# Projecting the keys and values of 14 context tiles in an earlier sublayer and keeping them in DRAM

## The chip, the cores and the metric

The kernel runs on one core of a Trainium2 chip. A core has a matrix engine (TensorE, PE in the profile), a vector engine (DVE), a scalar engine (ACT), GpSimd (POOL) and a queue that issues DMAs (SyncE, SP). Each runs its own instructions in a fixed order and waits on semaphores for the others. The time is microseconds on the device for one execution of the whole program; lower is better.

## The reference

A decoder of four layers with three sublayers each, on x of 64 sequences x 64 tokens x 256 channels; after each sublayer, x is layer-normalized with its residual. Sublayers are counted 1 to 12. These matter here:

```python
x = _layernorm(x + _L2_xattn_ref(64, 64, 256, L2_xattn_w, L2_xattn_u, x, ctx_2048), axis=-1)   # 8: a recurrence
x = _layernorm(x + _L2_ffn_ref(x, L2_ffn_weight, L2_ffn_bias), axis=-1)                         # 9: a quantized linear layer
x = _layernorm(x + _L3_attn_ref(x, ...), axis=-1)                                               # 10: self-attention
x = _layernorm(x + _L3_xattn_ref(x, ctx_2048, mask_1xSxS2_ff0, ...), axis=-1)                   # 11: cross-attention

def _L3_xattn_ref(hidden_states, encoder_hidden_states, attention_mask, Wq, bq, Wk, bk, Wv, bv, Wo, qn_w, kn_w):
    NH, NKV, HD = 16, 4, 128
    q = (hidden_states @ Wq + bq).reshape(b, s, NH, HD).transpose(0, 2, 1, 3)
    k = (encoder_hidden_states @ Wk + bk).reshape(b, se, NKV, HD).transpose(0, 2, 1, 3)
    v = (encoder_hidden_states @ Wv + bv).reshape(b, se, NKV, HD).transpose(0, 2, 1, 3)
    q, k = _rmsnorm(q, qn_w), _rmsnorm(k, kn_w)      # k and v then repeated for groups of 4 heads
    ...                                              # softmax(q k / sqrt(128) + mask) v
    return out @ Wo
```

The keys and values of sublayer 11 depend on the context alone, which is an input.

## The kernel before

The 4096 tokens are 8 groups of 4 tiles of 128 tokens (two sequences in a tile). `X[g]` holds the rows of a group, `CT[g]` the context of the group, transposed; both stay in SBUF. Large weights go through one ring of eight slots of 8 KB a partition (`weight`, `big_weight`); a slot is loaded again as soon as its last reader is done, and all loads are issued by SP in a fixed order. On PE the order is that of the Python code (`manual_schedule`); the order on the other engines comes from a scheduler at build time.

`l2_mix` computes sublayers 7 and 8: feed-forward slots (`hidden`, `down`), and beside them, as parts popped from a list `behind`, the recurrence of the group before. A recurrence takes the channels in two halves: keys are transposed (`keys`), a running maximum (`maximum`), exponential factors in the tile `e` on ACT (`factors`), two scans and a division on DVE (`sums`, `outputs`, `divided`). `finish` transposes the result back (`yx`), adds the residual and normalizes. The recurrence of the last group has no feed-forward beside it.

`l3_attentions` then computes sublayers 9 to 11. `linear.first` does sublayer 9 for group 0, whose result everything after waits for; the other groups' share (`parts`) runs inside sublayer 10. Sublayers 10 and 11 are one row of 64 + 64 steps; a step is one tile and half of its heads (`hb`). The stages of a step are spread over four turns of the loop by `do(stage, name)`: the projection of the queries at stage 0, turning queries and keys at 1, scores at 1, turning the probabilities and the values at 2, the output projection at 3. In sublayer 11, the step with `hb == 0` also projects the tile's keys (in `query`) and values (in `late`), in the banks of the queries:

```python
k = projected(cs(g, t), lambda c, n: w.kv[:, 0, c, n], slice(0, 512), w.bk, "k", 2)
```

`projected` is two matmuls of 128 x 512 in two PSUM banks used in turn, and an addition of the bias on DVE. In an even turn of the loop the second half of the queries comes ahead of the scores and the value projection near the end; in an odd turn the second half of the queries stands in that late place. The values are then copied by SP with the two sequences of the tile exchanged (`vs`), and keys are scaled on POOL.

In the trace's names, line 276 is `transpose4`, 270 the power on POOL that ends `rsqrt`, 1658 the matmul of `project`, and 255 and 257 the alternating copies of `copy`.

Of the kernel before, what the change touches and what calls it, by code (L numbers as in the profile page):

```python
# [19 lines left out]
P = 128  # L20
D = 256
S = 64
TG = 4
# [8 lines left out]
class Linear:  # L32
# [65 lines left out]
        ends = dec.normalized_parts(x, x)  # L98
        return [turn, quantized, lambda: tiles(0), lambda: tiles(2), *ends]

    def first(self, pool, bank):

        nc, dec = self.nc, self.dec
        x = dec.X[0]
        ps = [dec.transpose4([x[:, t, c * P : (c + 1) * P] for t in range(TG)], "xt") for c in range(2)]
        self.scales()
        xq = pool.tile([P, 2, NTOK], FP8, tag="xq8", name="xq8", bufs=1)
        y = pool.tile([P, TG, D], BF16, tag="s", name="y8f")
        mv = dec.smallp.tile([P, TG, 2], F32, tag="bnmv", name="bnmv", bufs=4)
        rstd, nb = dec.small(TG, "rstd", bufs=4), dec.small(TG, "nmr", bufs=4)  # L110

        def product(t):
            cols = slice(t * P, (t + 1) * P)
            for c in range(2):
                nc.vector.tensor_scalar(xq[:, c, cols], ps[c][:, cols], self.rxs, None, ALU.mult, saturate=False)
            if t % 2 == 0:
                self.banks = bank("o8").rearrange("p (t d) -> p t d", t=2)
            for c in range(2):
                nc.tensor.matmul(
                    self.banks[:, t % 2, :], xq[:, c, cols], self.wq[:, c, :], start=c == 0, stop=c == 1  # L120
                )
            nc.scalar.activation(y[:, t, :], self.banks[:, t % 2, :], AF.Copy, scale=self.sc)

        def rows(t):
            st = dec.smallp.tile([P, 6], F32, tag="bnst1", name="bnst1", bufs=4)
            r, b = rstd[:, t : t + 1], nb[:, t : t + 1]
            nc.vector.tensor_tensor(y[:, t, :], y[:, t, :], self.bias, ALU.add)
            nc.vector.tensor_tensor(x[:, t, :], y[:, t, :], x[:, t, :], ALU.add)
            nc.vector.bn_stats(st, x[:, t, :])
            nc.vector.bn_aggr(mv[:, t, :], st)  # L130
            dec.rsqrt(r, mv[:, t, 1:2], 1.0, 1e-5)
            nc.vector.scalar_tensor_tensor(b, mv[:, t, 0:1], -1.0, r, ALU.mult, ALU.mult)
            nc.scalar.activation(x[:, t, :], x[:, t, :], AF.Identity, bias=b, scale=r)

        for t in range(TG):
            product(t)
        for t in range(TG):
            rows(t)


class L1Ffn:
# [94 lines left out]
class Decoder:  # L236
# [1133 lines left out]
    def l2_l3(self, ctx):  # L1370

        shared = self.pool(ctx, "l2s", 1)
        linear = Linear(self, shared)
        for body in (self.l2_mix, self.l3_attentions):
            with ExitStack() as part:
                self.psum = self.pool(part, "psum_" + body.__name__, 2, space=PSUM, reuse_waits="tile")
                body(part, linear)

    def l2_mix(self, ctx, linear):
# [20 lines left out]

        nc.vector.tensor_scalar_mul(wqkv[:, :, :D], wqkv[:, :, :D], -1.0)
        es = [self.weight(f"l2x_e{i}").rearrange("p (i n) -> p i n", i=4) for i in range(2)]
        w, u = self.column("l2_w", 2), self.column("l2_u", 2)
        decay = wk.tile([P, 2, NB, S], F32, tag="decay", name="decay", bufs=1)
        for c in range(2):
# [197 lines left out]
        with self.tc.manual_schedule(engines={mybir.EngineType.PE}):  # L1605
            for part in mixing(0):
                part()
            slots = [(g, i) for g in range(self.n_groups) for i in range(HC)]
            parts, behind, done = [], [], []
            for n in range(len(slots) + 2):  # L1610
                if n < len(slots):
                    g, i = slots[n]
                    if i == 0:
                        parts = mixing(g + 1) if g + 1 < self.n_groups else []
                    hidden(g, i)
                if n >= 2:
                    down(*slots[n - 2])
                    if slots[n - 2][1] == HC - 1:
                        behind += [(n + 2, part) for part in recurrence(slots[n - 2][0])]

                        if slots[n - 2][0] == self.n_groups - 2:
                            behind[-1] = (len(slots) + 1, behind[-1][1])

                for _ in range(2 if n < len(slots) - HC else 3):
                    if behind and n >= behind[0][0]:
                        behind.pop(0)[1]()
                if parts:
                    parts.pop(0)()
            for _, part in behind:
                part()  # L1630

    def head_rms(self, wk, ps, out, eps, tag):
# [69 lines left out]
    def big_weight(self, name):  # L1702
# [11 lines left out]
            ws.append(w)  # L1714
        return ws

    def distances(self, pool):

        nc = self.nc
        half = lambda b: slice(b * S, (b + 1) * S)  # L1720
        dist = pool.tile([P, S], F32, tag="dist", name="dist", bufs=1)
        for b in range(2):
            nc.gpsimd.iota(
                dist[half(b)], pattern=[[1, S]], base=0, channel_multiplier=-1, allow_small_or_imprecise_dtypes=True
            )
        nc.vector.tensor_scalar_min(dist, dist, 0.0)
        bias = pool.tile([P, 16, S], F32, tag="bias", name="bias", bufs=1)
        start = 2.0 ** (-(2.0 ** -(math.log2(16) - 3)))
        for h in range(16):
            nc.vector.scalar_tensor_tensor(  # L1730
                bias[:, h, :], dist, start * start**h, self.causal64, ALU.mult, ALU.add
            )
        return bias

    def l3_attentions(self, ctx, linear):
# [7 lines left out]
        with self.tc.manual_schedule(engines={mybir.EngineType.PE}):  # L1743
            one, two = self.l3_attn(wk, steps, linear), self.l3_xattn(wk, steps)
            row = [(one, i) for i in range(n)] + [(two, i) for i in range(n)]
            for i in range(2 * n + 3):
# [30 lines left out]
                else:  # L1777
# [4 lines left out]
                    do(0, "query", 0)  # L1782
                    do(1, "key_turned")
                    do(1, "turn", 1)
                    odd = i % 2
                    if not odd:
                        do(0, "query", 1)
                    do(3, "outputs_turned")
                    do(3, "output")
                    do(1, "scores")  # L1790
                    do(2, "turned")
                    do(0, *(("query", 1) if odd else ("late",)))
                    do(2, "values")
                do(0, "end")
                if i == n - 2:
# [4 lines left out]
    def l3_attn(self, wk, steps, linear):  # L1800
# [3 lines left out]

        nc = self.nc
        EPS = 1e-5
        wq, wkk, wv, wp = (self.big_weight(n) for n in ("l3a_wq", "l3a_wk", "l3a_wv", "l3a_wproj"))
        qw, kw, sw = self.column("l3a_qw"), self.column("l3a_kw"), self.column("l3a_sw")
        both = wk.tile([P, 1], F32, tag="both", name="both", bufs=1)
        nc.vector.tensor_scalar(both, kw, qw, 1.0 / math.sqrt(P), ALU.mult, ALU.mult)  # L1810
# [146 lines left out]
                xts[g + 1] = self.transposed(self.X[g + 1], wk, "xt")  # L1957

        ahead, bank = [], lambda name: self.bank(name, bufs=2)
        linear.first(wk, bank)  # L1960
        bias = self.distances(wk)
        xts[0] = wk.tile([P, 2, NTOK], F32, tag="xt", name="xt")
        return SimpleNamespace(
# [4 lines left out]
    def l3_xattn(self, wk, steps):  # L1968
# [13 lines left out]

        def load():

            w.kv = self.weight("l3x_wkv").rearrange("p (i c n) -> p i c n", i=2, c=2)
            self.load(w.kv[:, 0], ins["l3x_wk"].rearrange("(c p) n -> p c n", p=P))
            self.load(w.kv[:, 1], ins["l3x_wv"].rearrange("(c p) n -> p c n", p=P))
            w.q = self.big_weight("l3x_wq")
            w.bq = self.weight("l3x_bq")
            self.load(w.bq, ins["l3x_bq"].broadcast_to([P, WCOLS]))  # L1990
# [8 lines left out]
            w.o = self.big_weight("l3x_wo")  # L1999

        half = lambda b: slice(b * S, (b + 1) * S)
        xts, zs, tiles, state = {}, {}, {}, {}

        def rms(x, out, name):

            sq = wk.tile([P, 4, P], F32, tag="sq", name="sq")
            nc.scalar.activation(sq, x, AF.Square)  # L2007
            nc.vector.tensor_reduce(out, sq, AX.X, ALU.add)
            self.rsqrt(out, out, 1.0 / P, EPS)

        def projected(lhs, w, cols, bias, tag, bufs):
            ps = self.bank("p", bufs=2)
# [5 lines left out]
        def query(i, u):  # L2018

            g, t, hb = steps[i]  # L2020
            if u == 0:
                state[i, "r"] = self.small(8, "hrq")
                if hb == 0:
                    k = projected(cs(g, t), lambda c, n: w.kv[:, 0, c, n], slice(0, 512), w.bk, "k", 2)
                    r = self.small(4, "hrk")
                    rms(k, r, "k")
                    nc.gpsimd.tensor_tensor(k, k, r.unsqueeze(2).broadcast_to([P, 4, P]), ALU.mult)
                    state[i, "k"] = k
# [7 lines left out]
        def late(i):  # L2036

            g, t, hb = steps[i]
            if hb == 0:
                v = projected(cs(g, t), lambda c, n: w.kv[:, 1, c, n], slice(0, 512), w.bv, "v", 2)  # L2040
                vs = wk.tile([P, 4, P], F32, tag="vs", name="vs")
                for b in range(2):
                    nc.sync.dma_start(out=vs[half(b)], in_=v[half(1 - b)])
                tiles[g, t, "v"] = v, vs
# [81 lines left out]
        def end(i):  # L2126
            g, t, hb = steps[i]
            if (t, hb) == (TG - 1, 0) and g + 1 < self.n_groups:
                rows(g + 1)

            if len(steps) - i in (12, 8):
                ahead.extend(self.l3_prepare(len(self.l3_rows)))
# [4 lines left out]
        cs = lambda g, t: lambda c: self.CT[g][:, c, t * P : (t + 1) * P]  # L2137
        return SimpleNamespace(
            load=load, load_biases=load_biases, load_output=load_output, rows=rows, turn=turn, query=query,
            late=late, key_turned=key_turned, turned=turned, scores=scores, output=output, values=values, end=end,  # L2140
        )

    def ternary(self, name):
# [224 lines left out]
```

## Time and profile before

| | us |
|---|---|
| median of 3 runs | 4365.31 |
| lowest, highest | 4363.7, 4369.8 |
| profiled execution | 4366.71 |
| its span, first to last instruction | 4365.0 |

| engine | busy us | share of the span | instructions |
|---|---|---|---|
| PE (matmuls) | 4079.3 | 93% | 28808 |
| DVE | 3095.2 | 71% | 6239 |
| ACT | 2005.0 | 46% | 3667 |
| POOL | 1465.4 | 34% | 1501 |

The page divides the span into 40 equal slices and shows, for each engine, its busy share of a slice in tenths; a row for PE's granted clock stands below them. Other views list one engine's instructions in order of time (start, duration, line, operation, output <- inputs, and in brackets the idle time before it and what ended that), or the busy time of all engines in chosen stretches. Matmul records of fp32 come in pairs: four records are one accumulation of two 128 x 512 products.

### The profile page before, as it was taken

What the parts mean: (1) busy time and instruction counts of PE and PEld (TensorE: products, weight loads), DVE (VectorE), ACT (ScalarE), POOL (GpSimd) and SP (SyncE); (2) the same over time, 40 slices, a digit from 0 to 9 for tenths busy, and PEclk for the clock granted to TensorE, in tenths of its full rate; (3) what the DMA queues carried; (4) which work ended last, traced back from release to release, by engine and by line L of the source; (5) the groups of instructions that cost most, each with busy time, mean ns of one, the idle gap of its engine ahead of it and who ended that gap; (6) DMA issues with size and microseconds to landing.
All of it is one profiled execution on the core that took longest, in us unless ns stands there. A gap on an engine that the chain in (4) does not pass through costs nothing. (4 is left out here: it accounts for less than half of the span.)

```text
span 4365.0 us, 73891 instructions
## 1 busy us (share of the span) xinstructions
PE 4079.3 (93%) x28808; PEld 2634.9 (60%) x28808; DVE 3095.2 (71%) x6239; ACT 2005.0 (46%) x3667; POOL 1465.4 (34%) x1501
## 2 busy tenths in 40 slices
PE   8889999989988999949999999999989999999898
PEld 5645566666665555526666666666656666666566
DVE  6744548888664687877777777777767777777676
ACT  5556545666423567544444444444422232232343
POOL 4411121332431111125555555555533334333111
PEclk9989998999999999979999999999999999999999
DMA  2200012333200000011111111111130000000000
GB/s 84 66 21 10 1 34 68 75 77 69 60 1 22 0 1 1 29 34 30 25 30 25 30 25 30 25 27 29 29 98 13 11 11 11 11 13 11 8 15 17
DMA packets 99685, 128.26 MB, mean 29 GB/s; under 512 B 14916, under 2 KB 72452, under 8 KB 97928
## 3 DMA queue, kind: packets, MB, share of 16 engines
q1 hardware_dynamic: 99336, 123.53, 11.4%
q8 instruction: 228, 3.74, 0.4%
q14 instruction: 121, 0.99, 0.1%
HBM read 61.87 MB, written 19.42 MB: 19 GB/s over the span
## 5 line engine op out<-in xcount | busy, mean ns | idle before, releaser
L270 POOL TENSOR_TENSOR hrq<-hrq,neg_half 128x4 f32<-128x4 f32 x256 | 258.3, 1009 | 535.6 <-DVE hrq L268 531.1
L270 POOL TENSOR_TENSOR rstd<-rstd,neg_half 128x4 f32<-128x4 f32 (+1 forms) x171 | 149.3, 874 | 716.8 <-DVE rstd L268 648.2
L1153 DVE TENSOR_REDUCE mc<-sq 128x2 f32<-128x512 f32 x512 | 317.2, 681 | 65.5 <-PE sk L1151 64.8
L1159 ACT ACTIVATE e<-sk 128x512 f32<-128x512 f32 x512 | 265.5, 608 | 113.2 <-PE sk L1151 111.8
L1148 PE MATMUL sq<-l1x 32*128 32x256 f32 x2048 | 277.0, 408 | 2.6 <-DVE mc L1153 1.6
L270 POOL TENSOR_TENSOR hrk<-hrk,neg_half 128x4 f32<-128x4 f32 x160 | 188.2, 1176 | 200.7 <-DVE hrk L268 197.5
L1658 PE MATMUL p<-l3a_wq,xt 128*128 128x512 f32 x512 | 244.6, 601 | 11.0 <-DVE v L257 9.9
L1151 PE MATMUL sk<-l1x 32*128 32x256 f32 x2048 | 253.2, 393 | 0.0
L1658 PE MATMUL p<-l3a_wk,xt 128*128 128x512 f32 x512 | 247.1, 605 | 0.0
L1148 PEld LDWEIGHTS sq<-l1x 32*128 32x128 f32 x2048 | 209.6, 195 | 57.3 <-issue 24.7
L1658 PE MATMUL p<-l3x_wq,xt 128*128 128x512 f32 x512 | 242.9, 597 | 0.3 <-DVE k L2015 0.3
L1658 PE MATMUL p<-l3a_wv,xt 128*128 128x512 f32 x512 | 234.0, 599 | 0.4 <-ACT y L94 0.4
L2111 PE MATMUL acc<-l3x_wo,yt 128*128 128x256 f32 x1024 | 232.3, 380 | 2.2 <-DVE yt L257 1.2
L1928 PE MATMUL acc<-l3a_wproj,yt 128*128 128x256 f32 x1024 | 234.0, 382 | 0.2 <-DVE yt L257 0.2
L1928 PEld LDWEIGHTS acc<-l3a_wproj,yt 128*128 128x128 f32 x1024 | 195.5, 191 | 54.0 <-issue 29.2
L2007 ACT ACTIVATE sq<-q 128x512 f32<-128x512 f32 x128 | 80.4, 628 | 296.4 <-DVE q L2015 251.5
L2111 PEld LDWEIGHTS acc<-l3x_wo,yt 128*128 128x128 f32 x1024 | 191.7, 190 | 40.9 <-issue 14.3
L1151 PEld LDWEIGHTS sk<-l1x 32*128 32x128 f32 x2048 | 188.6, 187 | 7.1 <-issue 2.9
L276 PEld LDWEIGHTS qT<-ident,q 128*128 128x128 f32 x1024 | 121.2, 141 | 107.2 <-issue 79.9
L276 PE MATMUL qT<-ident,q 128*128 128x128 f32 x1024 | 157.6, 277 | 12.7 <-ACT xt L255 7.9
L1912 POOL TENSOR_TENSOR hry<-hry,neg_half 128x8 f32<-128x8 f32 x64 | 106.3, 1661 | 183.7 <-DVE hry L1908 183.7
L1187 PE MATMUL ret<-e,vt 128*32 128x256 f32 x2048 | 140.9, 390 | 19.4 <-DVE mc L1153 18.3
(396 smaller groups left out, 10150.8 us busy)
## 6 DMA issues: line engine op xcount, KB each, us to landing
vs<-v SPq DMA_DIRECT2D x320, 128.0 KB
x<-in_x SPq DMA_DIRECT2D x8, 512.0 KB
ct<-in_ctxT SPq DMA_DIRECT2D x8, 512.0 KB
cn<-in_ctx SPq DMA_DIRECT2D x8, 512.0 KB
l1x<-in_ctx SPq DMA_DIRECT2D x128, 32.0 KB
l1x_x<-x SPq DMA_DIRECT2D x8, 512.0 KB
l1x<-l1x_x SPq DMA_DIRECT2D x128, 32.0 KB
l1x_r<-r SPq DMA_DIRECT2D x128, 32.0 KB
```

Of the source, the lines that this page charges most:

```text
L270: nc.gpsimd.tensor_tensor(out, out, self.neg_half[:, :n], ALU.pow)
L276: self.nc.tensor.transpose(ps[:, j * P : (j + 1) * P], blk, self.ident)
L1148: nc.tensor.matmul(ps[:, n, :], x_[rows, j, part], c_[rows, j, :], start=True, stop=True)
L1151: nc.tensor.matmul(ps[:, n, :], c_[rows, j, part], x_[rows, j, :], start=True, stop=True)
L1153: nc.vector.tensor_reduce(mc[new % 2][:, ra + k, 2 * j : 2 * j + 2], ps, AX.X, ALU.max, negate=True)
L1159: nc.scalar.activation(es[rb + k], ps, AF.Exp, scale=scale)
L1187: nc.tensor.matmul(ret[32 * r : 32 * r + 32, :], vt[i % 2][:, lc, 4 * r + j, :], es[r][:, lc, :], start=lc == 0, stop=lc == 1,)
L1658: self.nc.tensor.matmul(ps, lhs(c), w(c, cols), start=c == 0, stop=c == 1 and bias is None)
L1912: nc.gpsimd.tensor_tensor(r, r, self.neg_half[:, :8], ALU.pow)
L1928: nc.tensor.matmul(acc[:, :D], yts[h % 2][:, h // 2, :], wp[n // 8][:, (n % 8) * D : (n % 8 + 1) * D], start=n == 0, stop=n == 15,)
L2007: nc.scalar.activation(sq, x, AF.Square)
L2111: nc.tensor.matmul(acc[:, :D], yts[h % 2][:, h // 2, :], w.o[n // 8][:, (n % 8) * D : (n % 8 + 1) * D], start=n == 0, stop=n == 15,)
```

## The change

A new class `ContextRows` takes 14 of the 32 context tiles, every second one from the fourth on: (0,3), (1,1), (1,3), ... (7,1) as (group, tile). For each it makes two units, keys and values. A unit is the two matmuls, a copy from PSUM to SBUF on ACT, and a write of 256 KB to DRAM by SP, without the bias. `fill(n)` emits the next n units at the place in the code where it is called: 2 after the last feed-forward output, 2 ahead of the last group's recurrence, 17 ahead of its `finish`, 5 in `linear.first` after the transposition of `X[0]` and 2 after its products; 28 in all. The weights for this are loaded early into a ring slot of their own, and again for sublayer 11. The loads of the query and key weights of sublayer 10 stand earlier in the code, those of the value and output weights are where they were, one slot later in the ring.

In sublayer 11 the keys and values of such a tile are loaded from DRAM at the end of the step before and the bias is added on POOL in place. Where a tile's keys and values are loaded, the second half of the queries in its first step moves to the late place.

```diff
+    def fill(self, n, pool, tag, bufs, banks, copy):
+        dec = self.dec
+        while n and self.units:
+            n -= 1
+            g, t, i = self.units.pop(0)
+            ps = dec.bank("kv", bufs=banks)
+            for c in range(2):
+                dec.nc.tensor.matmul(
+                    ps, dec.CT[g][:, c, t * P : (t + 1) * P], self.w[:, i, c, :], start=c == 0, stop=c == 1
+                )
+            out = pool.tile([P, 512], F32, tag=tag, name="kv", bufs=bufs)
+            copy(out, ps)
+            dec.nc.sync.dma_start(out=self.dram[g, t, i], in_=out)
...
         ps = [dec.transpose4([x[:, t, c * P : (c + 1) * P] for t in range(TG)], "xt") for c in range(2)]
+        fill(5)
         self.scales()
...
         for t in range(TG):
             product(t)
+        fill(2)
         for t in range(TG):
             rows(t)
...
+        context.load()
+        fill = lambda n: context.fill(n, wk, "hid", 4, 3, nc.scalar.copy)
...
+                if n == len(slots) + 1:
+                    fill(2)
...
-            for _, part in behind:
+            fill(2)
+            self.l3a_qk = [self.big_weight(name) for name in ("l3a_wq", "l3a_wk")]
+            for k, (_, part) in enumerate(behind):
+                if k == len(behind) - 1:
+                    fill(17)
                 part()
...
-                    odd = i % 2
-                    if not odd:
+                    queries = i % 2 or i >= 2 * n or two.ready(i - n)
+                    if not queries:
                         do(0, "query", 1)
...
-                    do(0, *(("query", 1) if odd else ("late",)))
+                    if queries:
+                        do(0, "query", 1)
+                    if not i % 2:
+                        do(0, "late")
...
-        wq, wkk, wv, wp = (self.big_weight(n) for n in ("l3a_wq", "l3a_wk", "l3a_wv", "l3a_wproj"))
+        fill = lambda n: self.context.fill(n, wk, "q", 3, 2, nc.scalar.copy)
...
+        def ready(i):
+            return steps[i][:2] in context.tiles
+
+        def loaded(i):
+            for k, name in enumerate("kv"):
+                t = wk.tile([P, 4, P], F32, tag=name, name=name, bufs=2)
+                self.load(t.rearrange("p h d -> p (h d)"), context.dram[(*steps[i][:2], k)])
+                state[i, name] = t
+
+        def biased(i, name, bias):
+            t = state.pop((i, name))
+            flat = t.rearrange("p h d -> p (h d)")
+            nc.gpsimd.tensor_tensor(flat, flat, bias, ALU.add)
+            return t
...
+                    if ready(i):
+                        k = biased(i, "k", w.bk)
+                    else:
+                        k = projected(cs(g, t), lambda c, n: w.kv[:, 0, c, n], slice(0, 512), w.bk, "k", 2)
...
+            if hb == 1 and i + 1 < len(steps) and ready(i + 1):
+                loaded(i + 1)
```

The value path in `late` has the same choice between `biased` and `projected`.

More of the change, by code (lines that the diff above doesn't have):

```diff
@@ L99, in parts, with first @@
         return [turn, quantized, lambda: tiles(0), lambda: tiles(2), *ends]
-    def first(self, pool, bank):
+    def first(self, pool, bank, fill):
         nc, dec = self.nc, self.dec
@@ L136, in first, with __init__, load @@
             product(t)
+        fill(2)
         for t in range(TG):
             rows(t)
+class ContextRows:
+    def __init__(self, dec):
+        self.dec = dec
+        tiles = [(g, t) for g in range(dec.n_groups) for t in range(TG)][3::2][:14]
+        self.dram = {}
+        for g, t in tiles:
+            for i in range(2):
+                self.dram[g, t, i] = dec.tc.dram_tile([P, 512], F32, name=f"l3x_kv{i}_{g}_{t}")
+        self.units = list(self.dram)
+        self.tiles = set(tiles)
+    def load(self):
+        self.w = self.dec.keys_values_weight("l3x_wkv0")
+    def fill(self, n, pool, tag, bufs, banks, copy):
[11 more added lines that the diff above has]
+            dec.nc.sync.dma_start(out=self.dram[g, t, i], in_=out)
 class L1Ffn:
@@ L1375, in l2_l3 @@
         linear = Linear(self, shared)
+        self.context = ContextRows(self)
         for body in (self.l2_mix, self.l3_attentions):
@@ L1404, in l2_mix @@
         es = [self.weight(f"l2x_e{i}").rearrange("p (i n) -> p i n", i=4) for i in range(2)]
+        context = self.context
+        context.load()
+        fill = lambda n: context.fill(n, wk, "hid", 4, 3, nc.scalar.copy)
         w, u = self.column("l2_w", 2), self.column("l2_u", 2)
@@ L1715, in big_weight, with keys_values_weight @@
         return ws
+    def keys_values_weight(self, name):
+        w = self.weight(name).rearrange("p (i c n) -> p i c n", i=2, c=2)
+        for i, n in enumerate(("l3x_wk", "l3x_wv")):
+            self.load(w[:, i], self.ins[n].rearrange("(c p) n -> p c n", p=P))
+        return w
     def distances(self, pool):
@@ L1959, in l3_attn @@
         ahead, bank = [], lambda name: self.bank(name, bufs=2)
-        linear.first(wk, bank)
+        linear.first(wk, bank, fill)
+        (wq, wkk), wv, wp = self.l3a_qk, self.big_weight("l3a_wv"), self.big_weight("l3a_wproj")
         bias = self.distances(wk)
@@ L1983, in load @@
         def load():
-            w.kv = self.weight("l3x_wkv").rearrange("p (i c n) -> p i c n", i=2, c=2)
-            self.load(w.kv[:, 0], ins["l3x_wk"].rearrange("(c p) n -> p c n", p=P))
-            self.load(w.kv[:, 1], ins["l3x_wv"].rearrange("(c p) n -> p c n", p=P))
+            w.kv = self.keys_values_weight("l3x_wkv")
             w.q = self.big_weight("l3x_wq")
@@ L2001, in l3_xattn @@
         half = lambda b: slice(b * S, (b + 1) * S)
-        xts, zs, tiles, state = {}, {}, {}, {}
+        xts, zs, tiles, state, context = {}, {}, {}, {}, self.context
         def rms(x, out, name):
@@ L2023, in query @@
                 if hb == 0:
-                    k = projected(cs(g, t), lambda c, n: w.kv[:, 0, c, n], slice(0, 512), w.bk, "k", 2)
+                    if ready(i):
+                        k = biased(i, "k", w.bk)
+                    else:
+                        k = projected(cs(g, t), lambda c, n: w.kv[:, 0, c, n], slice(0, 512), w.bk, "k", 2)
                     r = self.small(4, "hrk")
@@ L2039, in late @@
             if hb == 0:
-                v = projected(cs(g, t), lambda c, n: w.kv[:, 1, c, n], slice(0, 512), w.bv, "v", 2)
+                if ready(i):
+                    v = biased(i, "v", w.bv)
+                else:
+                    v = projected(cs(g, t), lambda c, n: w.kv[:, 1, c, n], slice(0, 512), w.bv, "v", 2)
                 vs = wk.tile([P, 4, P], F32, tag="vs", name="vs")
@@ L2139, in l3_xattn @@
             load=load, load_biases=load_biases, load_output=load_output, rows=rows, turn=turn, query=query,
-            late=late, key_turned=key_turned, turned=turned, scores=scores, output=output, values=values, end=end,
+            late=late, ready=ready, key_turned=key_turned, turned=turned, scores=scores, output=output, values=values, end=end,
         )
```

## The prediction

> **What bounds the kernel now.** I read the page's 40 slices first, then busy time by stretch, then the engines in order of time at the seam and in one tile of the eleventh sublayer.
>
> ```profile
> PE   8889999989988999949999999999989999999898
> ...
> PEclk9989998999999999979999999999999999999999
> ```
>
> TensorE (PE) is at nine tenths nearly everywhere, so the kernel is bound by its matmuls. The one hole is the slice with a 4, where the granted clock is also 7: the seam between the eighth sublayer's last recurrence and the ninth sublayer. Busy time by stretch (columns: PE, weight loads, DVE, ACT, POOL, granted clock, DMA) sets the hole beside the steady part of the eleventh sublayer:
>
> ```profile
> 1854.20:1921.40 67.20, 11.69 (x44) 7.20 (x42) 51.83 (x122) 24.67 (x32) 6.20 (x13) 0.56 0.15 48
> 3240.00:4000.00 760.00, 742.76 (x5264) 500.96 (x5265) 573.41 (x1144) 223.09 (x392) 261.02 (x251) 1.00 0.06 12
> ```
>
> In the hole PE works 11.7 of 67.2 us at a mean clock of 0.56, while DVE works 52: the recurrence is a DVE chain. In the later stretch PE is busy 97.7%, DVE 75%, POOL 34%. PE's row in the hole, then one tile (two steps) of the eleventh sublayer:
>
> ```profile
> 1864.77 2.80 PE L1418 MATMUL tr<-ident,x 128*128 128x128 f32 x8 [3.99 <-ACT x L328]
> 1889.77 0.45 PE L1582 MATMUL yx<-ident,yx 128*128 128x128 f32 x1 [22.20 <-DVE yx L1571]
> 1899.18 1.75 PE L1582 MATMUL yx<-ident,yx 128*128 128x128 f32 x7 [8.96 <-DVE yx L1571]
> ...
> 1921.39 6.21 PE L1658 MATMUL p<-l3a_wq,xt 128*128 128x512 f32 x8 [1.13 <-ACT xt L255]
> ```
>
> ```profile
> 3520.86 0.66 PE L276 MATMUL qT<-ident,q 128*128 128x128 f32 x4
> 3521.35 1.88 PE L1658 MATMUL p<-l3x_wkv,ct 128*128 128x512 f32 x4
> 3523.07 1.88 PE L1658 MATMUL p<-l3x_wq,xt 128*128 128x512 f32 x4
> ...
> 3532.06 1.88 PE L1658 MATMUL p<-l3x_wkv,ct 128*128 128x512 f32 x4
> ...
> 3534.97 0.66 PE L276 MATMUL qT<-ident,q 128*128 128x128 f32 x4
> ...
> 3546.08 0.66 PE L276 MATMUL qT<-ident,q 128*128 128x128 f32 x4
> ```
>
> The first step of a tile, with key and value projection, takes 3534.97 − 3520.86 = 14.11 us, the second 11.11. Bracketless rows did not wait. Starts, not durations, give the price, since matmuls overlap: 3523.07 − 3521.35 = 1.72 us a projection.
>
> **What the change takes away.** For 14 of 32 tiles two projections leave this stage: 14 x 2 x 1.72 = 48.2 us of PE. The shortened first step, 14.11 − 3.44 = 10.67 us, holds the second step's PE work less one group of key transposes (0.43), with the second query in the same late place. The second step already runs unstalled at 11.11, which is why I expect the shortened one to stay on PE. DVE loses 28 bias additions of about 0.68 (19 us); per tile it had 0.754 x 25.22 = 19.0 us and keeps 17.7 in 21.8, 81%. Two covers get thinner: the probabilities were ready on POOL 4.7 us before their transposition in the odd step and 5.9 in the even one; the latter falls to 2.5. The late query's scale needs 5.0 us from its matmul through DVE, ACT, DVE and POOL; the next scores need it 8.9 us after that matmul, so 3.9 remain. Neither is used up, but DVE runs in a fixed order at 81%, and one wait of 0.25 us in a tile seems fair: **+3.5 us** (bounds 0, and 1.5 us a tile or 21).
>
> **What it puts on POOL and SP.** POOL adds 28 biases over two SBUF operands. Its nearest row:
>
> ```profile
> L2074 POOL TENSOR_TENSOR s<-s,smx x64: 1033/1044/1372, 3226.2 to 4051.5; 128x512 f32<-128x512 f32 x64
> ```
>
> 28 x 1.04 = 29 us, or 2.1 a tile; POOL goes from 8.6 to 10.7 in 21.8 us, off the path. The Trainium skill (SBUF, "Who interferes with whom") speaks against it: a DVE instruction with two SBUF inputs and a GpSimd one that reads SBUF exclude each other for a whole instruction. By that rule each addition could hold one DVE operation up to 1.04 us: 29 us of DVE, which at 19.8 of 21.8 us a tile would leave it almost bound and make the loss about 20 instead of 3.5. By the rows it is mostly POOL that waits: the multiplication above stretches from 1.03 to at most 1.37, while the mask addition on DVE (two SBUF inputs, 64 times) never exceeds 0.69. I take the rows. The value's addition waits for its load; behind it on POOL stand the key's scale and multiplication, which PE wants a step later. The load may go once values two tiles back are read, at the end of the step before; issue to use by an estimate is about 3 us (the seam's 1 MB weight loads take 5.2 to 5.5 from issue to use, of which some 3.3 us moved data, so about 2 fixed and 0.8 for 256 KB). It is covered by most of a step. On SP the 28 loads stand among swap copies that have a step to spare. No cost.
>
> **What it puts into the seam.** 28 units (a projection each, 1.72 us) are 48.2 us of PE in 67 us that PE had mostly free, plus an ACT copy of 0.58 (the row for `k<-tr`) and a 256 KB write each. Their places decide, so I follow ACT's new fixed order:
>
> ```profile
> 1876.49 1.91 ACT L1551 ACTIVATE l2x_e<-l2x_e 128x2048 f32<-128x2048 f32 x1
> ...
> 1900.61 2.00 ACT L1951 ACTIVATE l3a_wproj<-l3a_wproj,l3a_sw 128x2048 f32<-128x2048 f32 x1 [8.80 <-DMA l3a_wproj<-in_l3a_wproj]
> ```
>
> - Before the first exponential ACT now runs one copy and the second half's first Relu (1.06): the half's sums on DVE start 0.6 + 1.06 = 1.7 us later. DVE waited 2.65 us for it and has nothing else, so the last `yx` is ready at 1899.1 + 1.7 = 1900.8.
> - With three banks PE stops at unit 10 (1877) until ACT has finished the exponentials' preparation (1881.6), then runs at 1.72 to unit 21 at 1901.4: 0.6 after `yx`. That 4.6 us gap may halve the clock again (it fell about 4 us after PE stopped at 1854.2), costing 1.7 more; I leave that to the range.
> - The five units behind the transposes wait for copies that stand behind the normalization on ACT; the quantized product starts 2.3 us late. Two more copies go ahead of the last normalization: query projection at 1924.5, 3.1 late.
> - Against it: PE is now warm. The first eight matmuls took 6.21 at half clock; eight such in the same stage at full clock take 3.6. That returns 2.6.
> - The second output weight now takes the slot of the moved weights, so it is loaded only after unit 28 (1921.4) and lands near 1926.9. ACT scales it (2.0) ahead of the first squares, to 1928.9, where the squares began at 1925.9 before. Behind it wait the second query's copy and, through the bank, PE; following both to the first key transposes leaves 0.5 to 1.5.
> - SP: the two value weight loads and the first output weight queue among the writes; the value weight lands near 1892 and is wanted at 1944. Four output buffers allow 6.9 us for a write, against about 3.
>
> Net in the seam **+1.5 us**. Bounds: −3 if the warm clock repays more, +12 if the clock falls, writes come slowly and ACT holds the first step. The early load of the moved weights takes a slot that its last reader leaves before the loads next to it; its DMAs precede results that are used a sublayer later. No cost.
>
> **Sum.** The profiled execution took 4366.7 us (span 4365.0), 1.4 over the median shown. 4366.7 − 48.2 + 3.5 + 1.5 = 4323.5, against the median 4322: I say 4323.
>
> **Rivals.**
> 1. *The shortened step stalls.* For: DVE at 81% in a fixed order, the POOL/DVE exclusion. Against: the second step runs so already. With 1.5 us a tile the 3.5 becomes 21: about 4340.
> 2. *The seam gives part back*, by the clock, slow writes or ACT behind the last weight. For: ACT and SP run in order, and the weight is loaded late. Against: the hole is longer than the work. At +12 instead of +1.5: about 4333.
> 3. *Slower: the late query's scale decides the step.* Its operations on POOL now queue behind key bias, value bias and key multiplication. If these delay it past the 3.9 us left, DVE stands at the scores' scaling with all evacuations behind it, and PE stops on its two projection banks. Each tile loses what exceeds 3.9; beyond 3.9 + 3.44 = 7.3 us a tile the change loses. At 8 us: 14 x 4.1 − 48.2 + 1.5 = +11, 4377. POOL's added 2.1 us a tile are far from it.
> 4. *Nothing moves*: the stage falls back on another bound of the same length. 4366; the step of 11.11 us speaks against it.
>
> **How the numbers follow.** Likeliest 60%, its own range 4315 to 4331; rival 1 19%, rival 2 14%, rival 3 4%, rival 4 3%. The range takes in both milder rivals: 4313 to 4344. Within 0.2% (8.7 us, about what a measurement of this kernel can tell from no change) lies rival 4 alone, beyond it upward rival 3.
>
> **What would show it.** Right: steps with loaded keys start 10.7 us apart in PE's row; the slice with 4 becomes 8 or 9 and its clock 9 or 10; the first query projection runs 8 matmuls in about 3.6; PE's busy sum hardly changes. Wrong: PE waiting on DVE or POOL in those steps, DVE two-input operations above 0.69, a long ACT wait for the second output weight, `yx` transposes well past 1902. A time above 4344 refutes the forecast.

## The result, and the profile after

| | before | after |
|---|---|---|
| median, us (4 runs each, same chip) | 4365.82 | 4338.98 |
| lowest, highest | 4363.7, 4369.8 | 4336.5, 4343.85 |
| profiled execution, us | 4366.71 | 4343.85 |
| its span | 4365.0 | 4342.1 |

The ratio after/before is 0.9939, 95% interval 0.9922 to 0.9956: 27 us faster, where 42 were forecast. The profiled execution of after is the longest of its four, so the profiles differ by 22.9 us only; against the forecast sum for the profiled execution (4323.5) 20.3 us are missing. The question is where they are.

The line of busy times and the slices from the page of after:

```profile
PE 4079.0 (94%) x28788; PEld 2635.7 (61%) x28808; DVE 3092.6 (71%) x6211; ACT 2018.1 (46%) x3695; POOL 1498.3 (35%) x1529
...
PE   8889998989888999989999999999989999999898
...
PEclk9989999999999999999999999999999999999999
```

The slice with the 4 is an 8 now, and its clock a 9. PE does the same work as before (4079.3 us), so the hole was filled and not merely moved. A detail to keep: DVE lost 28 bias additions of 0.68 us, or 19 us, and yet it is busy for 3092.6 us instead of 3095.2. The same two stretches as before, by windows:

```profile
1854.20:1921.40 67.20, 56.14 (x155) 25.91 (x154) 51.01 (x115) 34.49 (x53) 4.11 (x10) 0.97 0.43 152
3240.00:4000.00 760.00, 726.91 (x5316) 501.31 (x5312) 589.11 (x1151) 228.75 (x405) 301.65 (x287) 0.99 0.09 23
```

In the seam PE works 56 us instead of 12, at a clock of 0.97. In the eleventh sublayer it works 726.9 of 760 us instead of 742.8: this stage was limited by PE and is so no longer everywhere. PE's row in the seam:

```profile
1882.40 20.85 PE L168 MATMUL kv<-l3x_wkv,ct 128*128 128x512 f32 x44 [4.26 <-ACT kv L172]
1903.09 1.04 PE L1621 MATMUL yx<-ident,yx 128*128 128x128 f32 x8
...
1925.43 3.70 PE L1703 MATMUL p<-l3a_wq,xt 128*128 128x512 f32 x8 [1.29 <-ACT xt L290]
```

The first query projection starts at 1925.4 instead of 1921.4 and takes 3.70 us instead of 6.21. The first key transposes come at 1936.54 instead of 1934.05: the seam ends 2.5 us later, of which 0.8 were there before its first unit.

Now the steps of the eleventh sublayer. A step is here the stretch of PE's row, one turn of the loop, that holds the step's own projections; it begins with a group of query transposes. I took these starts from both traces, from tile 2 of group 0 on, and sorted the differences of 59 step lengths, after minus before, by tile of the group and step of the tile:

| tile | first step, us | second step, us |
|---|---|---|
| 0 | 0.0 | 0.0 |
| 1 (keys and values loaded in 7 groups) | −24.0 | **+21.4** |
| 2 | +0.5 | +2.4 |
| 3 (loaded in 7 groups) | −25.5 | 0.0 |

The sum is −25.2, where −44.7 was forecast. The shortened steps gain what they should (7 x 3.43 in tile 1). Nearly all that tile 1 gains is given back in one place, its second step. PE's row there, in group 1:

```profile
3337.23 0.66 PE L311 MATMUL qT<-ident,q 128*128 128x128 f32 x4
...
3345.00 1.88 PE L1703 MATMUL p<-l3x_wq,xt 128*128 128x512 f32 x4
...
3347.90 0.66 PE L311 MATMUL qT<-ident,q 128*128 128x128 f32 x4
...
3350.12 0.60 PE L311 MATMUL kT<-ident,k 128*128 128x128 f32 x4
3352.95 0.66 PE L311 MATMUL qT<-ident,q 128*128 128x128 f32 x4 [2.23 <-DVE qT L292]
3353.45 5.31 PE L2189 MATMUL acc<-l3x_wo,yt 128*128 128x256 f32 x16
...
3363.16 0.66 PE L311 MATMUL qT<-ident,q 128*128 128x128 f32 x4
```

The shortened step takes 3347.90 − 3337.23 = 10.67 us, to the digit of the forecast. The next takes 15.26 instead of 11.60: PE waits 2.23 us for a DVE copy, and then sixteen matmuls that take 3.62 us at full clock take 5.31. The view in windows of 1 us says why (the number ahead of the last two is the granted clock):

```profile
3354.00:3355.00 1.00, 1.00 (x5) 0.79 (x4) 0.35 (x3) 0.86 (x2) 1.00 (x2) 0.62 0.00 0
3355.00:3356.00 1.00, 1.00 (x4) 0.80 (x3) 0.77 (x2) 0.00 (x0) 0.78 (x2) 0.50 0.00 0
3356.00:3357.00 1.00, 1.00 (x4) 0.73 (x3) 0.00 (x0) 0.00 (x0) 0.89 (x1) 0.50 0.00 0
3357.00:3358.00 1.00, 1.00 (x5) 0.85 (x4) 0.00 (x0) 0.00 (x0) 0.00 (x0) 0.67 0.00 0
```

From 1.3 us behind the wait on, PE's clock is halved for 3.4 us, which costs 1.7 us more. PE waits 2.2 us for that copy in all seven groups; in four of them the clock falls, in three it does not (those steps are 13.57, 13.56 and 14.64 us).

Why is DVE late? DVE and then POOL in the same tile, and behind them `rstd` and its reader in that place before:

```profile
3341.19 0.87 DVE L303 TENSOR_SCALAR hrk<-hrk 128x4 f32<-128x4 f32 x1
...
3344.67 0.71 DVE L303 TENSOR_SCALAR rstd<-bnmv 128x4 f32<-128x4 f32 x1
...
3347.33 1.38 DVE L342 TENSOR_SCALAR x<-z,bnmv,rstd 128x256 f32<-128x256 f32 x4 [1.36 <-POOL rstd L305]
...
3352.22 0.68 DVE L292 COPY qT<-qT 128x512 f32<-128x512 f32 x1
```

```profile
3340.99 1.04 POOL L2152 TENSOR_TENSOR s<-s,smx 128x512 f32<-128x512 f32 x1
3341.99 1.27 POOL L2080 TENSOR_TENSOR v<-v,biases 128x512 f32<-128x512 f32 x1
3343.22 1.02 POOL L305 TENSOR_TENSOR hrk<-hrk,neg_half 128x4 f32<-128x4 f32 x1
3344.31 1.04 POOL L2102 TENSOR_TENSOR k<-k,hrk 128x512 f32<-128x512 f32 x1
3345.31 1.01 POOL L305 TENSOR_TENSOR hrq<-hrq,neg_half 128x4 f32<-128x4 f32 x1
3346.28 1.01 POOL L305 TENSOR_TENSOR rstd<-rstd,neg_half 128x4 f32<-128x4 f32 x1
```

```profile
3350.90 1.01 POOL L270 TENSOR_TENSOR rstd<-rstd,neg_half 128x4 f32<-128x4 f32 x1 [0.89 <-DVE rstd L268]
...
3351.94 1.38 DVE L307 TENSOR_SCALAR x<-z,bnmv,rstd 128x256 f32<-128x256 f32 x4 [0.52 <-POOL rstd L270]
...
3353.89 0.66 PE L276 MATMUL qT<-ident,q 128*128 128x128 f32 x4
...
3356.97 0.65 PE L276 MATMUL qT<-ident,q 128*128 128x128 f32 x4 [0.27 <-DVE qT L257]
```

Three things meet in this turn of the loop. First, the layer normalization of the group before falls here (statistics, `rstd`, four scalings): its last output comes three turns after the last step of that group, which is the turn of tile 1's first step. Second, POOL's value bias stands in a chain of six operations without a gap, with `rstd` at its end, and DVE, in order, waits 1.36 us for it (0.52 in the same place before). Third, two small DVE operations on 128x4 take 0.87 and 0.71 us instead of 0.16 and 0.17. Each ends within 0.03 us of the end of a large POOL instruction that began before it (3342.06 and 3342.03; 3345.38 and 3345.35). The same operation over the stage, before and then after (smallest, median and largest duration in ns):

```profile
L268 DVE TENSOR_SCALAR hrk<-hrk x29: 152/158/163, 3267.4 to 3995.1; 128x4 f32<-128x4 f32 x29
```

```profile
L303 DVE TENSOR_SCALAR hrk<-hrk x30: 157/740/871, 3268.1 to 3995.8; 128x4 f32<-128x4 f32 x30
```

From 3270 to 4000 us DVE's scaling operations of this kind take 50.9 us instead of 29.6. That is where the 19 us of saved additions went.

But the third thing is not what PE waits for here. POOL takes the results of the two held operations only 1.2 and 0.9 us after they are done, and both end before DVE's wait of 1.36 us: without the hold that wait would be longer, and nothing else. What PE waits for is `rstd`. Before, it ended 1.98 us ahead of the second step (3350.90 + 1.01 against 3353.89) and PE waited 0.27 us; now it ends 0.61 us ahead (3346.28 + 1.01 against 3347.90) and PE waits 2.23. Of the 1.96 us more, 1.37 are the later `rstd`; the other 0.6 are one more DVE operation between it and the copy, a sum of squares of the late second queries. The experiments below change when `rstd` ends, and PE's wait follows it.

### The profile page after: what moved, and what is told of

The parts are those of the page before. It is cut to its first block, busy times and chain, and to the rows that moved or that the text cites. A ratio compares the mean times of both kernels' runs of the same rounds, so it can differ in the third digit from the quotient of the medians.

```text
span 4342.1 us, 74081 instructions
## 1 busy us (share of the span) xinstructions
PE 4079.0 (94%) x28788; PEld 2635.7 (61%) x28808; DVE 3092.6 (71%) x6211; ACT 2018.1 (46%) x3695; POOL 1498.3 (35%) x1529
## 3 DMA queue, kind: packets, MB, share of 16 engines
q14 instruction: 124, 1.01, 0.1%
## 5 line engine op out<-in xcount | busy, mean ns | idle before, releaser
L1703 PE MATMUL p<-l3a_wq,xt 128*128 128x512 f32 x512 | 242.1, 595 | 11.1 <-DVE v L292 9.9
```

Of the source, the lines that this page charges most:

```text
L1703: self.nc.tensor.matmul(ps, lhs(c), w(c, cols), start=c == 0, stop=c == 1 and bias is None)
```

## The experiments

All edits are to the changed kernel unless said otherwise; each median stands beside a kernel before of the same chip, and the ratio is to that one. "The stage" is the sum of the 59 step differences to before in the profile, −25.2 us for the change.

**The seam alone.**

```diff
-        self.tiles = set(tiles)
+        self.tiles = set()
```

> The 28 units are projected and written as in the change, but sublayer 11 does not use them: it projects all keys and values itself, with the loop order of before. This prices the earlier part alone. By the forecast the seam costs 1.5 us: about 4367 us. If the missing 16 us lie in the seam: about 4380. If the warm clock repays more than the delays cost: 4363.

Measured: 4369.04 against 4367.66 us, ratio 1.0002, interval 0.9994 to 1.0010, so +1 us with −3 to +4 around it. The seam's price is about as forecast, and the missing 16 us are not there.

**Other tiles.** Two kernels: tiles 2 and 3 of groups 0 to 6, and the same row one tile later (`[1:15]` for `[:14]`).

```diff
-        tiles = [(g, t) for g in range(dec.n_groups) for t in range(TG)][3::2][:14]
+        tiles = [(g, t) for g in range(dec.n_groups) for t in (2, 3)][:14]
```

> The same 14 tiles' worth of work, but tiles 2 and 3 of groups 0 to 6 in place of tiles 1 and 3. Theory A (the layer normalization of the group before, which falls on DVE in the loop turn of tile 1's first step, finds no room once that step is shortened): the shortened steps of tile 2 take 10.7 us and the step behind each 11.1, tile 1's second step goes back from 15.2 to 11.6, and the 21 us lost there come back: about 4318 us. Theory B (any shortened first step overloads DVE's fixed order, with the bias additions on POOL): the second step of tile 2 stretches to 15 us as tile 1's did, and the time stays at about 4339.

> Tiles 2 and 3 again, but beginning with tile 3 of group 0 and ending with tile 2 of group 7, so that no loaded tile lies in the first turns of sublayer 11, where the kernel with tiles 2 and 3 waited 7.0 us for POOL's probabilities instead of 5.6 and lost 3.7 us over three turns. If that loss came from the two tiles' bias additions on POOL at that place: 3 to 4 us less than with tiles 2 and 3, about 4326. If it came from elsewhere: 4329 again.

Measured: 4329.33 (ratio 0.9911, 0.9897 to 0.9926) and 4328.28 us (ratio 0.9905, 0.9890 to 0.9920). The stage gives −39.2 and −40.9. Tile 2 in PE's row of the second kernel:

```profile
3363.36 0.66 PE L311 MATMUL qT<-ident,q 128*128 128x128 f32 x4
...
3374.03 0.66 PE L311 MATMUL qT<-ident,q 128*128 128x128 f32 x4
...
3377.04 0.66 PE L311 MATMUL qT<-ident,q 128*128 128x128 f32 x4 [0.20 <-DVE qT L292]
...
3385.56 0.66 PE L311 MATMUL qT<-ident,q 128*128 128x128 f32 x4
```

The step behind the shortened one takes 11.53 us, not 15, and the wait for DVE is 0.20 instead of 2.23. The same step, shortened in the same way, is harmless where no normalization falls: theory A stands, B falls. It is about 10 us short of the fall to 4318 that was expected: in the profile of the first kernel the second steps of tile 2 are still 6.0 us longer than before (0.4 in most, and one half-clock stretch), and those of tile 1, in three groups, 4.4. Of the three first turns of sublayer 11 the later row saves 2.85 us in the profile (59.2 instead of 62.05); the times can't tell the two apart.

**The normalization emitted later.**

```diff
-                if t == TG - 1:
+                if t == TG - 1 and g == self.n_groups - 1:
                     self.layernorm(x, z)
...
+            if (t, hb) == (1, 1) and g:
+                self.layernorm(self.X[g - 1], zs[g - 1])
```

> Tiles 1 and 3 as in the change, but the layer normalization of the finished group (statistics, rstd, four scalings) is emitted two turns of the loop later, ahead of tile 2's first step, which still projects keys and values and takes 14.1 us. Theory A: tile 1's second step falls from 15.2 to between 11.1 and 12.5 us, and the time to about 4320 us. Theory B: no change in that step, about 4339.

Measured: 4347.32 us, ratio 0.9950 (0.9936 to 0.9963); the stage gives −20.0. This test missed its aim: the order on DVE is made by the scheduler, which put the statistics and `rstd` back where their input was ready, with the same wait of 1.36 us, and only spread the four scalings between the other operations; PE's wait grew to 2.64 us. It says nothing on A or B.

**The biases left out, and the value bias on DVE.**

```diff
-            nc.gpsimd.tensor_tensor(flat, flat, bias, ALU.add)
+            (nc.vector if name == "v" else nc.gpsimd).tensor_tensor(flat, flat, bias, ALU.add)
```

(The other kernel drops the line; it leaves out the bias of the loaded keys and values.)

> Leaves out the bias of the loaded keys and values, so POOL loses 28 additions of 1.27 us. Theory C (the value bias, which stands on POOL ahead of the key's scale, holds rstd and so DVE): tile 1's second step loses most of its 3.6 us excess, and the time falls by 15 to 20 us, to about 4321. Theory A (DVE is full in that tile whatever POOL does): POOL's chain gets 1.3 us shorter, so at most 7 x 1.3 = 9 us come back, to 4330 to 4335.

> Tiles 1 and 3 as in the change; the bias of the loaded values is added on DVE instead of POOL, that of the keys stays on POOL. DVE gets 14 additions of about 0.69 us, POOL loses 14 of 1.27. Theory C (POOL's chain in tile 1's first step, in which the value bias stands ahead of the key's scale, the late query's scale and rstd, holds DVE): tile 1's second step falls from 15.2 to about 12.9 us as it did without biases, and its half-clock stretch goes: about 4332 us. Theory A (DVE itself is full there): 0.7 us more of DVE in that tile make the step longer than 15.2, and the time 4341 to 4346.

Measured: 4333.65 us without biases (ratio 0.9915, 0.9901 to 0.9930), 4347.23 with the value bias on DVE (ratio 0.9953, 0.9940 to 0.9965, which overlaps the interval of the change). Without biases tile 1's second step takes 12.85 us, as C said, and the stage gives −34.0, the 9 us that A allowed. With the value bias on DVE the step stays at 15.02, where C said 12.9 and A more than 15.2, and tile 3's first step grows from 12.67 to 13.64. Tile 1 of group 1 without biases, then with the value bias on DVE:

```profile
3345.25 1.01 POOL L305 TENSOR_TENSOR rstd<-rstd,neg_half 128x4 f32<-128x4 f32 x1 [0.20 <-DVE rstd L303]
...
3347.58 0.66 PE L311 MATMUL qT<-ident,q 128*128 128x128 f32 x4
...
3351.91 0.66 PE L311 MATMUL qT<-ident,q 128*128 128x128 f32 x4 [1.52 <-DVE qT L292]
```

```profile
3343.82 1.52 POOL L2102 TENSOR_TENSOR k<-k,hrk 128x512 f32<-128x512 f32 x1
...
3346.65 1.01 POOL L305 TENSOR_TENSOR rstd<-rstd,neg_half 128x4 f32<-128x4 f32 x1 [0.20 <-DVE rstd L303]
...
3348.50 0.66 PE L311 MATMUL qT<-ident,q 128*128 128x128 f32 x4
...
3353.31 0.66 PE L311 MATMUL qT<-ident,q 128*128 128x128 f32 x4 [2.00 <-DVE qT L292]
```

Both take an addition of 1.27 us out of POOL's chain, but `rstd` ends only 0.71 and 0.23 us sooner (1.32 and 0.84 us ahead of the second step instead of 0.61), because POOL now waits 0.20 us for DVE's input of it. In both a scaling of the queries is held 1.0 us on DVE ahead of that input; in the second kernel DVE also has the addition (0.68 us), and POOL's key multiplication takes 1.52 us beside it in all 14 places, 1.04 in the change. So POOL's chain and DVE's fixed order limit `rstd` in turn, and a shorter chain on POOL is worth little if DVE pays for it. Neither C alone nor A alone describes this.

**The small scaling on ACT.** This takes the small scalings of the sums of squares off DVE and leaves POOL's operations as they are.

```diff
-            self.rsqrt(out, out, 1.0 / P, EPS)
+            nc.scalar.activation(out, out, AF.Copy, scale=1.0 / P, bias=EPS)
+            nc.gpsimd.tensor_tensor(out, out, self.neg_half[:, : out.shape[-1]], ALU.pow)
```

> The change with one edit: in sublayer 11 the small operation that scales the sums of squares ahead of the power (128x4, a TENSOR_SCALAR on DVE) is done by ACT; POOL's chain, bias additions included, stays. Theory D (these small operations are held on DVE while a POOL instruction runs, 0.74 us instead of 0.16 for the keys' one, and DVE is full in tile 1's turn): DVE loses some 46 us in the stage, tile 1's second step falls from 15.2 to 12.5 us or less, without a half-clock stretch, and the time to about 4325. Theory C (the length of POOL's chain decides): tile 1's second step stays above 13.5, and the time at 4338 or more, since ACT adds a hop to each scale.

> The kernel before, with the small scaling of sublayer 11 on ACT and nothing else. Its DVE has room in every tile; only tile 1's second step (11.6 instead of 11.1 us) can shorten: 8 x 0.5 us or 4 us at most, 4362 to 4366. Much less than 4360 would mean that the small operations were a cost by themselves and not only beside the shortened steps.

Measured: 4329.68 us, ratio 0.9909 (0.9895 to 0.9922), so some 13 us below the change; on the kernel before, the same edit gives 4371.00, ratio 1.0006 (0.9998 to 1.0014), no gain. PE, POOL and DVE of the first in tile 1 of group 1:

```profile
3336.68 0.66 PE L311 MATMUL qT<-ident,q 128*128 128x128 f32 x4
...
3347.35 0.66 PE L311 MATMUL qT<-ident,q 128*128 128x128 f32 x4
...
3351.65 0.66 PE L311 MATMUL qT<-ident,q 128*128 128x128 f32 x4 [1.49 <-DVE qT L292]
3352.15 3.62 PE L2190 MATMUL acc<-l3x_wo,yt 128*128 128x256 f32 x16
```

```profile
3338.57 1.01 POOL L2066 TENSOR_TENSOR hrq<-hrq,neg_half 128x4 f32<-128x4 f32 x1 [6.91 <-ACT hrq L2065]
3339.69 1.04 POOL L2153 TENSOR_TENSOR s<-s,smx 128x512 f32<-128x512 f32 x1
...
3344.99 1.01 POOL L305 TENSOR_TENSOR rstd<-rstd,neg_half 128x4 f32<-128x4 f32 x1
```

```profile
3346.03 1.38 DVE L342 TENSOR_SCALAR x<-z,bnmv,rstd 128x256 f32<-128x256 f32 x4 [1.14 <-POOL rstd L305]
```

PE's wait shrinks to 1.49 us, the clock does not fall in any of the seven groups, and the step takes 12.83 us, a little above the 12.5 expected; the stage gives −37.4. So the edit helps, but the trace does not give theory D's reason. DVE still waits 1.14 us for `rstd`, so DVE's time ahead of it is not what is short. What has moved is the start of POOL's chain: ACT delivers the first sum of squares sooner, POOL has taken its power by the time the next operation's input is there, and the multiplication behind it starts 3.01 us after the step's start (3339.69 against 3336.68) instead of 3.76. From there POOL works without a gap as before, and `rstd` ends 0.74 us sooner. The four kernels side by side, in tile 1:

| kernel | `rstd` ends ahead of the second step, us | PE waits in it, us |
|---|---|---|
| the change | 0.61 | 2.23 |
| value bias on DVE | 0.84 | 2.00 |
| without biases | 1.32 | 1.52 |
| small scaling on ACT | 1.35 | 1.49 |

The two columns add up to 2.84 in each, within 0.02 in all seven groups: DVE does the same work from the end of `rstd` to the copy, and 5.7 us pass until PE goes on. So PE's wait is set by the end of POOL's `rstd`. The 12 us that the stage regains are seven times 0.74 us and four half-clock stretches of 1.7. That the held operations cost time by themselves is not shown: the kernel before gains nothing from the edit, and neither does the kernel with tiles 2 and 3 (below). What is left of tile 1's loss (9.3 of 21.4 us) is the normalization itself and POOL's chain.

**The second queries in their old place.**

```diff
-                    queries = i % 2 or i >= 2 * n or two.ready(i - n)
+                    queries = i % 2 or i >= 2 * n
```

> Undoes one part of the change: in steps with loaded keys and values the second half of the queries stays ahead of the scores, so that nothing stands between the turned probabilities and the values on PE. Where the last turns of the row have nothing there, PE waits 0.73 us for the copy of the probabilities. If only that wait is exposed: 14 x 0.73 us or 10 us, about 4350. If the early place spares DVE's chain in tile 1 instead (the second query's scale is then ready earlier): under 4335.

Measured: 4342.76 us, ratio 0.9940 (0.9928 to 0.9953), the same as the change. Tile 1's shortened step takes 11.42 instead of 10.67 us (the exposed copy, 0.75), and its second step 12.74 instead of 15.26 without a fall of the clock, since two DVE operations fewer stand between `rstd` and the copy (4.6 us from the end of `rstd` to PE's transposes instead of 5.7): both expectations were half right, and they cancel. The reordering brought nothing here.

**Combinations.**

> Tiles 2 and 3 (from group 0's tile 3 on) and the small scaling on ACT. If D holds: tile 2's second step goes from 11.5 to 11.1 us and tile 1's first steps keep the normalization under 14.1, so the stage comes within 5 us of the full 48 us: about 4322. If ACT's hop delays the scales: 4330 or more.

> Tiles 2 and 3 from group 0's tile 3 on, and the bias of the loaded values on DVE. If both effects are separate and DVE has room in tiles 2 and 3: 2 to 4 us below the kernel with the tiles alone, about 4323. If DVE is the tighter one there: equal or up to 5 us above it.

> Tiles 2 and 3 of all eight groups: 16 tiles, 32 units, the four more of them ahead of the transposition of the last recurrence's result. In the traces with 28 units PE runs there without a gap until that result is ready (unit 21 ends at 1903 us, the transposition follows at once). If the hole is full: four units of 1.72 us put everything behind them 6.9 us later, sublayer 11 gets 6.9 us shorter, and with the first two tiles' 3.7 us the time is 4328 to 4332, no gain over 14 tiles. If there is still room: about 4322.

The last kernel's edit is `for t in (2, 3)]` without a limit, and `fill(21)` for `fill(17)`. Measured, in this order: 4328.25 (ratio 0.9907, 0.9894 to 0.9921), 4350.91 (0.9955, 0.9942 to 0.9967) and 4331.53 us (0.9928, 0.9914 to 0.9941). The small scaling on ACT adds nothing once the tiles are 2 and 3: tile 2's second step stays at 11.53 us, where D expected 11.1. The value bias on DVE costs 22 us there, far more than the 5 expected: tile 2's second step grows from 11.5 to 12.4 us and more, and tile 3's first step from 12.7 to 13.6. And the hole is full: with four more units the transposition of the recurrence's result starts 57.0 us after the first unit instead of 48.1 in the change, so 8.8 us later, and the stage gains only 6.5 us more than with 14 tiles (−45.7 against −39.2).

So the kernels with 14 tiles 2 and 3 (4328 to 4329 us) beat both, by 38 to 42 us against before and, by the ratios, 12 to 15 against the change.

## Why the prediction was right, and where it was off

The direction and the mechanism were right, and the time fell in the range, but at the place of the first rival ("the shortened step stalls", about 4340), not of the likeliest case. By its steps:

- **The projections that leave.** −48.2 us was right for the steps themselves: 10.67 us against a forecast of 10.67.
- **The term that failed: +3.5 us for waits in the shortened steps**, "one wait of 0.25 us in a tile seems fair". The runs show 23.0 in the profile, 21.4 of it in tile 1's second step. The working took DVE's mean over the tiles (81%) and asked whether a mean tile has room, and it put POOL's added work "off the path". The normalization's operations don't fall in a mean tile; they all fall in the turn of tile 1's first step, which was one of the two chosen for shortening, and there POOL is on the path: `rstd` stands at the end of its chain, DVE waits for it, and PE for DVE. The trace of before showed the place: tile 1's second step took 11.61 us there and tile 2's 11.11.
- **POOL beside DVE: "I take the rows".** The Trainium skill (SBUF, "Who interferes with whom") names two kinds of DVE instruction that share a port with GpSimd: those with two SBUF inputs, and those in a two-port mode, which `tensor_scalar` can enter; whoever issues first has the port for the whole instruction. I looked at the first kind alone (the mask addition; one of 64 takes 0.82 us after the change, the others 0.69 at most). The second kind is held: of 160 small scalings in sublayer 11, 49 take between 0.35 and 0.87 us (before, 28 of 155 take 0.35), and each of them ends within 0.06 us of the end of a POOL instruction. The prediction put the hold at up to 29 us of DVE by the rule; measured are 50.9 − 29.6 = 21. From this hold the rule's working made a loss of about 20, near the 23.0 above; that agreement is luck, since in tile 1 the hold falls into time that DVE would otherwise wait for `rstd`.
- **What a stall starts.** The sum had no term for PE's clock in sublayer 11. A wait of 2.2 us was followed by half clock for 3.4 us in four groups of seven, 1.7 us each. In the last steps the clock halved too and sixteen matmuls took 5.52 us instead of 3.88, which lost 1.6 more after the stage; the waits there (0.73 and 1.16 us) stand in before as well, without a fall.
- **POOL's additions** took 1.27 us each, not the 1.04 of the row for a multiplication by a broadcast operand.
- **The seam: +1.5 us.** The profile shows +1.7 (2.5 less the 0.8 from before it), and the seam alone +1 in the times. The details held: PE stopped for 4.26 us at 1878 (forecast: 4.6), the first query projection began at 1925.4 (1924.5) and took 3.70 us (3.6). The clock did halve at that stop, from 1883.1 to 1886.5, which the prediction had left to the range; the end of the block of units came at 1903.2 instead of 1901.4.
- **The late place of the second queries** was part of the shortened step's 10.67 us. The gain doesn't depend on it: in the old place the time is the same.
- **The rest.** The three turns at the border of sublayers 10 and 11 became 1.8 us shorter. The sum for the profile: 4323.5 + 19.5 (steps) + 1.0 (seam) − 1.8 + 1.6 = 4343.8, against 4343.85.

Rival 3 named POOL's queue behind the two biases as the danger and the late query's scale as what it delays. The queue was there, but the operation at its end that mattered was the normalization's `rstd`, and the size of the loss was rival 1's.

## What to carry to other kernels

A mean busy share over a stage says little about a step that is to be shortened: list what the other engines do in that very step, above all the work that comes once per group, and take the time out of steps in which the next engine has nothing extra. When work goes to an engine that is off the path on average, look at what else stands behind it in that step and who waits for it: here one operation of 1.0 us at the end of POOL's chain set PE's wait. A DVE operation that grows beside POOL is a loss only where DVE does not wait afterwards anyway. And when PE's wait nears 2 us, add the half clock that may follow it: in four of seven groups here it made 2.0 us of loss into 3.6.

## What was not expected of the hardware

A gap of 2.2 us in PE's work was enough to halve its clock in four of seven like places, 3.4 us long each time. It did not have to: gaps of 2.28 and 2.25 us in sublayer 11 of before left the clock full. The Trainium skill (TensorE: Matmul & The Clock Gate, Part 1) states a fall after an idle window of about 3.4 us; here shorter gaps did it, sometimes, and the gap of 4.26 us in the seam did it too. Over all fourteen traces, in sublayer 11 without its first and last turns, none of 36 gaps from 1.3 to 1.8 us was followed by a fall, and 27 of 48 from 1.87 to 2.64 us were. The fall in the last turns of the change, behind gaps of 0.73 and 1.16 us close together, stays unexplained.
